# Layer 1's values directly behind its scores, inside the second unit of layer 2's values

## The chip, the core and the metric

The kernel runs on one core of a Trainium2 chip. Its time is the device time in microseconds (us) of one execution, and the numbers compared are medians of several executions. Engines are named as in the profile: PE is TensorE's matmul, PEld its weight load, DVE is VectorE, ACT is ScalarE, POOL is GpSimd and SP is SyncE. L1234 is line 1234 of the kernel.

## What is computed

The input x has four images of 64x64 positions with 64 channels. Four attention layers follow each other, each over the 4096 positions of an image. Layer 1, which the change touches, has few channels in its scores (8) and its values (32), and its keys and values are pooled to 1024 positions:

```python
# layer 0: attention over 4096 keys, 64 channels
x = gamma * softmax(q @ k) ... + x
# layer 1
theta = x @ sn(w_theta)                     # 4096 x 8
phi   = maxpool2(x @ sn(w_phi))             # 1024 x 8
attn  = softmax(theta @ phi.T)              # 4096 x 1024
g     = maxpool2(x @ sn(w_g))               # 1024 x 32
x     = x + sigma * ((attn @ g) @ sn(w_o) + b_o)
# layer 2: group norm, attention over 4096 keys, projection, + x
# layer 3: group norm, attention over 4096 keys, projection, + normed x
```

sn divides a weight matrix by an estimate of its largest singular value. All is float32. The softmax is computed as exponentials of the scores, values times exponentials, and a division by the sum of the exponentials.

## The kernel before

Of each image, the core holds arrays of 128 partitions: two halves of the positions by 64 channels. Layers 0, 2 and 3 are written as a sequence of *steps*. The big attention of the foreground gives each step two *units*. A unit is 128x1024 scores, built by four matmuls in 64x64 corners of TensorE (`first`, L1199 for layers 2 and 3, L971 for layer 0), their exponentials on ScalarE (L1204), their sums into `zacc` on VectorE (L1210), and two or more steps later the values times exponentials (`then`, L1234 for layers 2 and 3), again four matmuls, into two PSUM accumulators. A chunk of 512 queries has 32 units j = 0..31; there are four chunks, so 64 steps.

Everything else is background work in small pieces. It is a Python generator that yields the *place* it wants for its next piece, and `step` lets it go on at that place. A step issues its instructions in this order:

- the two score units of the foreground;
- the first unit of values;
- place MID: one piece of background work, or a piece of urgent work of the foreground itself;
- the second unit of values; if the background waits for place LATE, this unit is split into query columns 0 to 255 and 256 to 511, and the background's piece goes between them. For j = 0 and j = 31 `parts` doesn't split: the piece goes behind the whole unit;
- the functions in the list `later` (VectorE work put off to here);
- place END.

A place ALONE takes the MID slot and keeps LATE empty for that step. [...]

Layer 1 is such background work. `layer1(on, st, bank)` runs for image 0 beside layer 0 with `bank` False, and for images 1, 2 and 3 beside layer 2 of the image before with `bank` True. In both cases it goes through 16 units (j, k): two halves j of the queries, eight blocks k of 128 keys. For unit n:

- `scores(j, k)` takes two score tiles, fills them with eight matmuls of 8 rows by 64 columns of the array (L1079), and issues two exponentials on ScalarE (L1085). It returns a function `accumulate` that adds both to the sums on VectorE (L1094).
- `add(j, k)` multiplies the pooled values with the exponentials of that unit: four matmuls of 128 rows by 32 columns (L1105), into one PSUM accumulator over the eight k where `bank` is True. At k = 7 ScalarE copies the accumulator out (L1116).
- behind `add` of the last k of the first half, `finish(0)` starts with `normalise`: four matmuls sum the exponentials over partitions (L1121), ScalarE copies that out (L1127), and reciprocals (L1130) and a product follow in pieces at MID.

A unit's scores go at LATE, and the values of the unit before it at END of the same step. Score tiles come from a pool of two [...], shared by foreground and background; the PSUM accumulators from a pool of four; the exponentials from a pool of 14.

Of the kernel before, what the change touches and what calls it, by code (L numbers as in the profile page):

```python
# [597 lines left out]
def fast_path(tc: tile.TileContext, a: dict, out: bass.AP, bad):  # L598
# [21 lines left out]
    MID, ALONE, LATE, END = range(4)  # L620
# [153 lines left out]
    later = []  # L774
# [256 lines left out]
    def layer1(on, st, bank):  # L1031
# [39 lines left out]
        def scores(j, k):  # L1071

            ss = [s_tile() for e in range(2)]
            n, d = divmod(k, 2)
            for m in range(2):
                for e in range(2):
                    for i in range(2):
                        r = slice((2 * e + i) * 32, (2 * e + i) * 32 + D8)
                        nc.tensor.matmul(  # L1079
                            ss[e][half(m), chunk(i)], pgs[0 if e == d else 1][r, ds(n * P + m * C, C)],  # L1080
                            th[r, chunk(2 * j + i)], start=True, stop=True,
                        )
            ps[j, k] = pk = [p_tile() for e in range(2)]
            for e in range(2):
                nc.scalar.activation(pk[e], ss[e], AF.Exp)  # L1085
            if k == 0:
                return lambda: None
            if k == 1:
                zaccs[j] = x_tile("zacc1").rearrange("p (e f) -> p e f", e=2)
            zs = [ps[j, 0][e] if k == 1 else zaccs[j][:, e, :] for e in range(2)]  # L1090

            def accumulate():
                for e in range(2):
                    nc.vector.tensor_tensor(zaccs[j][:, e, :], zs[e], pk[e], ALU.add)  # L1094

            return accumulate

        def add(j, k):
            if k == (NK - 1 if bank else 0):
                os[j] = o_tile("o1")  # L1100
            if k == 0 and bank:
                accs[j] = acc_tile()
            acc = accs[j] if bank else s_tile()[:, 0:512]
            for q in range(4):
                nc.tensor.matmul(  # L1105
                    acc[quarter(q), :], g[:, k, :], ps[j, k][q // 2][:, chunk(q % 2)],
                    start=(k == 0 or not bank), stop=(k == NK - 1 or not bank),
                )
            if k > 0:
                del ps[j, k]  # L1110
            if k == 1:
                del ps[j, 0]
            if not bank and k > 0:
                nc.vector.tensor_tensor(os[j], os[j], acc, ALU.add)
            elif not bank or k == NK - 1:
                nc.scalar.copy(os[j], acc)  # L1116
# [27 lines left out]
        def finish(j):  # L1144

            if not bank:
                yield ALONE
            yield from normalise(j)
            yield MID
            yield ALONE  # L1150
            last(j)

        end = None
        todo = [(j, k) for j in range(2) for k in range(NK)]
        for n in range(len(todo) + 1):
            accumulate = None
            if n < len(todo):
                yield LATE
                accumulate = scores(*todo[n])
            if n:  # L1160
                yield END
                add(*todo[n - 1])
            if accumulate:
                accumulate()
            if n == NK:
                end = finish(0)
                at = next(end)
            elif end is not None:
                yield at
                at = next(end, None)  # L1170
                end = end if at is not None else None
# [535 lines left out]
    layer0(s0)  # L1707
    drain()
    background(3.0, layer1("DVE", s0, False), before2("DVE", s0))
    free = layer0(s1)  # L1710
    drain()
    background(3.0, layer1("ACT", s1, True), before0("ACT", s2))
    free = layer2(s0, free)
    drain()
    background(1.0, before2("DVE", s1), loads(s3))
    free = layer0(s2)
    drain()
    background(3.0, layer1("ACT", s2, True), before0("ACT", s3))
    free = layer2(s1, free)
    drain()  # L1720
# [97 lines left out]
```

## Time and profile before

| what | value |
|---|---|
| median of 3 runs | 3004.53 us (3003.02 to 3005.59) |
| the profiled execution | 3005.78 us |
| its span, first to last instruction | 3003.7 us |
| TensorE clock granted, mean | 0.999 |
| layer 1 scores L1079 beside layer 2 start at | 586.64, 1096.44, 1606.23 us |
| VectorE busy from 584 to 700 us | 92.84 of 116 us |
| ScalarE busy from 584 to 700 us | 75.40 of 116 us |

The span is cut by the foreground: layer 0 of image 0 first, then a turn of layer 2 or 3 of one image and layer 0 of another. The part with layer 1 beside layer 2 is about 105 us long and comes three times. Within it TensorE's records follow each other almost without idle time (115.29 us of 116 between 584 and 700).

How to read the timeline of TensorE: one line is a run of equal instructions, with the start, the length, the line of the kernel, what is written and read, the shape and the number of records. Every matmul of this kernel leaves two records of its shape. The length of a line [...] overlaps the next line; differences between starts are the times that blocks take.

### The profile page before, as it was taken

How to read it: one execution, taken by the hardware profiler on the slowest of the kernel's cores; microseconds unless marked ns; L12 is line 12 of the kernel's file. 1: busy time of each engine (PE TensorE's matmuls, PEld its weight loads, DVE VectorE, ACT ScalarE, POOL GpSimd, SP SyncE). 2: the span in 40 equal slices, each digit the busy share in tenths (PEclk: the TensorE clock that was granted, in tenths of full speed). 3: DMA queues.
4: the chain of work that ended last, by engine and by line, in shares of the span. 5: the costliest groups of instructions: out<-in, count | busy, mean ns of one | idle time of the engine just before them, and what ended most of it. 6: DMA issues, size and time to landing. Idle time of an engine off the chain costs nothing.

```text
span 3003.7 us, 64700 instructions
## 1 busy us (share of the span) xinstructions
PE 2979.2 (99%) x28509; PEld 1133.0 (38%) x28509; DVE 1760.1 (59%) x2003; ACT 1943.8 (65%) x2816; POOL 34.1 (1%) x32
## 2 busy tenths in 40 slices
PE   9999999999999999999999999999999999999998
PEld 4333233433444433344443333333343334333333
DVE  1211332587731068772017887777887777877777
ACT  6877778666588866557886655655555655555554
POOL 0000000000000000000000000000000000000000
PEclk9999999999999999999999999999999999999999
DMA  2010000000001000000000000000000000000000
GB/s 37 2 29 5 1 1 2 19 2 1 15 1 29 1 5 1 15 2 10 7 2 5 2 8 9 19 5 8 5 19 6 17 1 1 12 12 5 9 5 9
DMA packets 42081, 25.79 MB, mean 9 GB/s; under 512 B 39872, under 2 KB 39872, under 8 KB 40384
## 3 DMA queue, kind: packets, MB, share of 16 engines
q1 hardware_dynamic: 40080, 21.17, 3.7%
q8 instruction: 225, 3.69, 0.5%
q10 hardware_dynamic: 1712, 0.41, 0.1%
q14 instruction: 64, 0.52, 0.1%
HBM read 4.79 MB, written 4.19 MB: 3 GB/s over the span
## 4 chain that ended last, share of the span: by engine, by line
PE 98%; ACT 1%; SPq 0%; DVE 0%; issue 0%; DMA 0%; ACTq 0%; DVEq 0%
PE acc L1234 30%; PE s L1199 30%; PE acc L996 15%; PE s L971 14%; PE s L1079 2%; PE acc L1105 1%; ACT p L1085 1%; PE s L883 1%; PE s L1105 1%; PE s L1262 1%; PE s L1346 0%; PE s L902 0%; PE s L1260 0%; PE s L1443 0%; PE s L1366 0%; PE s L1051 0%
## 5 line engine op out<-in xcount | busy, mean ns | idle before, releaser
L1204 ACT ACTIVATE p<-s 128x1024 f32<-128x1024 f32 x1024 | 994.8, 1022 | 705.6 <-PE s L1199 694.0
L1210 DVE TENSOR_TENSOR zacc<-zacc,p 128x1024 f32<-128x1024 f32 x960 | 1174.1, 1223 | 372.2 <-ACT p L1204 334.4
L975 ACT ACTIVATE p<-s 128x1024 f32<-128x1024 f32 x512 | 519.9, 1016 | 42.7 <-PE s L971 24.3
L1234 PE MATMUL acc<-p,v 64*64 64x512 f32 (+1 forms) x4456 | 525.2, 558 | 0.0
L996 PE MATMUL acc<-p,vs 64*64 64x512 f32 (+1 forms) x4224 | 512.2, 578 | 0.5 <-ACT vs L985 0.5
L1199 PE MATMUL s<-q,k 64*64 64x512 f32 x2048 | 495.5, 593 | 2.1 <-ACT p L1085 2.1
L1234 PE MATMUL acc<-p,hT 64*64 64x512 f32 x4096 | 494.1, 590 | 0.0
L971 PE MATMUL s<-xT,q 64*64 64x512 f32 x2048 | 487.4, 591 | 2.5 <-DVE v L903 0.6
L971 PE MATMUL s<-xT,q_swapped 64*64 64x512 f32 x2048 | 488.4, 591 | 0.0
L1199 PE MATMUL s<-q,xT 64*64 64x512 f32 x2048 | 486.9, 589 | 0.0
L1199 PE MATMUL s<-q,h_swapped 64*64 64x512 f32 x2048 | 479.4, 589 | 0.0
L1199 PE MATMUL s<-q,k_swapped 64*64 64x512 f32 x2048 | 477.6, 593 | 0.0
L977 DVE TENSOR_REDUCE all_z<-z 128x1 f32<-128x4 f32 x128 | 20.1, 157 | 643.2 <-ACT p L975 643.2
L1234 PEld LDWEIGHTS acc<-p,v 64*64 64x64 f32 x4456 | 179.9, 133 | 285.0 <-issue 280.0
L996 PEld LDWEIGHTS acc<-p,vs 64*64 64x64 f32 x4224 | 176.3, 133 | 270.3 <-issue 206.5
L985 ACT ACTIVATE vs<-v,all_r 64x64 f32<-64x64 f32 x512 | 177.2, 346 | 145.2 <-PE acc L996 72.4
L1234 PEld LDWEIGHTS acc<-p,hT 64*64 64x64 f32 x4096 | 156.7, 133 | 263.8 <-issue 263.1
L971 PEld LDWEIGHTS s<-xT,q_swapped 64*64 64x64 f32 x2048 | 145.8, 133 | 146.3 <-issue 114.2
L1199 PEld LDWEIGHTS s<-q,h_swapped 64*64 64x64 f32 x2048 | 143.9, 133 | 141.2 <-issue 135.5
L971 PEld LDWEIGHTS s<-xT,q 64*64 64x64 f32 x2048 | 145.8, 133 | 134.1 <-issue 106.0
L1199 PEld LDWEIGHTS s<-q,xT 64*64 64x64 f32 x2048 | 143.4, 133 | 140.1 <-issue 137.7
L1199 PEld LDWEIGHTS s<-q,k 64*64 64x64 f32 x2048 | 140.1, 132 | 148.3 <-issue 100.2
(233 smaller groups left out, 1560.2 us busy)
## 6 DMA issues: line engine op xcount, KB each, us to landing
k_swapped<-k SPq DMA_DIRECT2D x8, 512.0 KB, 6.0
h_swapped<-xT SPq DMA_DIRECT2D x8, 512.0 KB, 5.3
out_dram<-turned SPq DMA_DIRECT2D x62, 64.0 KB, 1.9
xin<-in_x_dram SPq DMA_DIRECT2D x24, 128.0 KB, 5.0
q_swapped<-q SPq DMA_DIRECT2D x6, 512.0 KB, 5.4
pg<-pg SPq DMA_DIRECT2D x8, 128.0 KB, 2.3
xin<-in_x_dram SPq DMA_DIRECT2D x12, 64.0 KB, 2.3
xin<-in_x_dram ACTq DMA_DIRECT2D x4, 64.0 KB, 2.6
```

Of the source, the lines that this page charges most:

```text
L883: nc.tensor.matmul(bank[i][half(e), :], w[half(i), half(e)], rhs[half(i), chunk(2 * j + (1 - e if exchanged else e))], start=True, stop=True,)
L971: nc.tensor.matmul(s[half(e), chunk(i)], queries(m, i, e), k[half(i), chunk(c)], start=True, stop=True)
L975: nc.scalar.activation(p, s, AF.Exp, accum_out=zs[m][:, c : c + 1])
L985: nc.scalar.activation(vs[half(e), :], v[half(e), m, :], AF.Copy, scale=rz[half(e), m : m + 1])
L996: nc.tensor.matmul(acc[c][half(i), cols], vs[half(e), :], ps[2 * t + n][half(e), chunk(i)][:, cols], start=(m == 0 and e == 0), stop=(m == ...
L1079: nc.tensor.matmul(ss[e][half(m), chunk(i)], pgs[0 if e == d else 1][r, ds(n * P + m * C, C)], th[r, chunk(2 * j + i)], start=True, stop=True,
L1085: nc.scalar.activation(pk[e], ss[e], AF.Exp)
L1105: nc.tensor.matmul(acc[quarter(q), :], g[:, k, :], ps[j, k][q // 2][:, chunk(q % 2)], start=(k == 0 or not bank), stop=(k == NK - 1 or not ...
L1199: nc.tensor.matmul(s[half(e), chunk(i)], k[(j + i) % 2][half(i), ds(j // 2 * P + e * C, C)], q[half(i), chunk(c)], start=True, stop=True,)
L1204: nc.scalar.activation(p, s, AF.Exp)
L1210: add = lambda: nc.vector.tensor_tensor(zaccs[c], p0, p, ALU.add)
L1234: nc.tensor.matmul(accs[c][e][half(i), cols], v[half(e), j, :], p[half(e), chunk(i)][:, cols], start=(j == 0), stop=(j == NB - 1),)
```

## The change

```diff
@@ layer1
         for n in range(len(todo) + 1):
             accumulate = None
             if n < len(todo):
                 yield LATE
                 accumulate = scores(*todo[n])
             if n:
-                yield END
+                if not bank:
+                    yield END
+                elif n == len(todo):
+                    yield LATE
                 add(*todo[n - 1])
-            if accumulate:
+            if accumulate and bank:
+                later.append(accumulate)
+            elif accumulate:
                 accumulate()
             if n == NK:
                 end = finish(0)
                 at = next(end)
```

Where `bank` is True, the values of unit n - 1 (`add`) are issued right behind the scores of unit n, at the same LATE, so between the two parts of the second unit's values, and no longer at END. The last unit's values, which have no scores ahead of them, ask for a LATE of their own. The accumulation of the exponentials goes into `later`, which the same step works off behind the second unit's values. With `add` of unit 7, the start of `finish(0)` moves from END to LATE as well. Where `bank` is False, nothing changes.

## The prediction

> **What bounds the kernel now.** I read the page first, its busy table and the chain that ended last.
>
> ```profile
> PE 2979.2 (99%) x28509; PEld 1133.0 (38%) x28509; DVE 1760.1 (59%) x2003; ACT 1943.8 (65%) x2816; POOL 34.1 (1%) x32
> ...
> PE 98%; ACT 1%; SPq 0%; DVE 0%; issue 0%; DMA 0%; ACTq 0%; DVEq 0%
> ```
>
> TensorE is busy 99% of the span and is 98% of the chain. So a rearrangement elsewhere is worth nothing, and even on TensorE nothing is won by filling idle time. What can change is the time that TensorE loses while it counts as busy. To see that, I read the timeline of TensorE over one step that carries a piece of layer 1 beside layer 2. Columns: start, length, instructions. The lengths overlap, so I take differences of starts.
>
> ```profile
> 659.41 1.11 PE L1079 MATMUL s<-th,pg 8*64 8x512 f32 x16
> 660.46 0.66 PE L1234 MATMUL acc<-p,v 64*64 64x256 f32 x8
> 661.05 1.06 PE L1105 MATMUL acc<-p,pg 128*32 128x512 f32 x8
> 662.05 0.65 PE L1199 MATMUL s<-q,k 64*64 64x512 f32 x2
> ...
> 663.81 1.47 PE L1234 MATMUL acc<-p,v 64*64 64x512 f32 x16
> 665.21 1.15 PE L1079 MATMUL s<-th,pg 8*64 8x512 f32 x16
> ```
>
> From one layer 1 score block to the next: 1.05 (scores) + 0.59 (rest of the second unit's values) + 1.00 (layer 1's values) + 1.76 (two score units of layer 2) + 1.40 (the first unit's values and half of the second's) = 5.80 us. The lines give each matmul as two records. Eight such 64x64 records of 512 columns with nothing of another shape around them take 0.86 us (649.56 to 650.42), and the sixteen of two units 1.72 us (697.08 to 698.80). By that measure the five blocks would take 0.86 + 0.43 + 0.86 + 1.72 + 1.29 = 5.16. The missing 0.64 us sits at the borders between tile shapes: 8*64, 64*64, 128*32 and 64*64 again, with four borders a step.
>
> Then two other places of the same timeline. In the first, 128*32 is followed by 64*64 values; in the second the layer 1 scores are followed directly by layer 1's values, because there the second unit is the last of its chunk and isn't split.
>
> ```profile
> 693.46 1.07 PE L1121 MATMUL acc<-zacc,ones 128*32 128x512 f32 x8
> 694.46 1.09 PE L1234 MATMUL acc<-p,v 64*64 64x512 f32 x8
> 695.37 0.60 PE L1199 MATMUL s<-q,k 64*64 64x512 f32 x2
> ...
> 627.36 1.11 PE L1079 MATMUL s<-th,pg 8*64 8x512 f32 x16
> 628.40 1.07 PE L1105 MATMUL acc<-p,pg 128*32 128x512 f32 x8
> 629.62 0.65 PE L1199 MATMUL s<-q,k 64*64 64x512 f32 x2 [0.15 <-ACT p L1085]
> ```
>
> Last, what releases TensorE after a layer 1 score block: the timelines of weight loads and of ScalarE in the next step, and the weight loads and VectorE where layer 1 sums its first half's denominators.
>
> ```profile
> 668.46 0.14 PEld L1199 LDWEIGHTS s<-q,k_swapped 64*64 64x64 f32 x2 [0.38 <-ACT p L1085]
> ...
> 666.47 1.94 ACT L1085 ACTIVATE p<-s 128x1024 f32<-128x1024 f32 x2 [1.27 <-PE s L1079]
> ```
>
> ```profile
> 634.94 0.12 PEld L1121 LDWEIGHTS acc<-zacc,ones 128*32 128x32 f32 x2 [0.30 <-issue]
> ...
> 635.14 0.11 PEld L1121 LDWEIGHTS acc<-zacc,ones 128*32 128x32 f32 x2
> ...
> 633.87 1.22 DVE L1094 TENSOR_TENSOR zacc<-zacc,p 128x1024 f32<-128x1024 f32 x1
> ```
>
> The second score unit's weights (668.46) go out just as the second layer 1 exponential ends (666.47 + 1.94 = 668.41). And the last two of the denominators' weight loads (635.14) go out just after the last layer 1 accumulation ends (633.87 + 1.22 = 635.09): that wait is already near its point.
>
> [...] a border costs 0.10 to 0.19 us, no border nothing. [...] within one shape (the weight loads for the layer 2 values run 0.43 us ahead of their matmuls, 663.39 against 663.81), and shows none of it over a border: the load for L1105 starts at 661.05 with its matmul. [...]
>
> **The change part by part.**
>
> 1. *Layer 1's values move from the step's end to directly behind the scores.* What moves is four matmuls (eight records); in one step an image ScalarE's copy L1116 goes with them, behind the same two exponentials as before; nothing of it is on SP's or POOL's queue, and no DMA. No instruction is added or removed in a normal step. TensorE's order was values-half, scores, values-half, layer 1 values, next scores of layer 2; it becomes values-half, scores, layer 1 values, values-half, next scores. The borders go from four to three, since the last two blocks now have one shape. With rows from above: scores before 128*32, 1.04 (627.36 to 628.40); 128*32 before 64*64 values, 1.00 (693.46 to 694.46); the half behind it, 0.43 plus the 0.05 to 0.06 by which the block at 694.46 exceeds 0.86, so 0.49; two score units without a border ahead, 1.71 (695.37 to 697.08); and 1.40. Sum 5.64 to 5.65: 0.15 us less a step.
>
> 2. *How many steps.* Each image has 16 layer 1 units of scores, so 15 steps with both scores and values. One of them (627.36) has the unsplit second unit, and its order on TensorE stays as it is. One (632.85) also starts the denominators and goes by itself below. That leaves 13. Images 1, 2 and 3 run layer 1 beside layer 2 (first score blocks at 586.64, 1096.44, 1606.23, with the same steps): 39 steps x 0.15 = 5.85 us less. Layer 1 of image 0, beside layer 0, keeps its order.
>
> 3. *The last values wait for LATE, not END.* That step (687.05: 1.82, 1.00, 1.77) now splits the second unit: 1.40 + 1.00 + 0.49 + 1.71 = 4.60 against 4.59. Four matmuls more, nothing in time.
>
> 4. *The denominators' matmuls of the first half (L1121) move forward with the values.* They were issued at 635.37 (632.85 + 1.04 + 0.60 + 0.88). Without the 0.60 they would start at 634.77, but the accumulation they read ends at 635.09, and their last two weight loads can't go before 635.14. VectorE can't be earlier: it waits at 631.00 for ScalarE's copy of layer 2's accumulator, and then works without a gap to 635.09. So TensorE stands some 0.36 us. From 635.14: 1.00 to the half, 0.49, 1.71 gives 638.34 to 638.35 against 638.11 in the trace: 0.24 us later, three times, 0.72 us more. Behind the waiting instruction TensorE's queue holds the half of layer 2's values and the next scores; those feed ScalarE, which has its copies L1116 and L1127 to do in that time and slack behind them.
>
> 5. *Accumulations go through the list of later work instead of directly.* They come behind that list's other entries as before, in the same step: VectorE's order doesn't change. Cost nothing. Its cover: steps with a reciprocal hold about 5.55 us of VectorE work in 5.80 (idle 0.20 to 0.24), and would still fit in 5.65. If they didn't, only the accumulators would lag, which TensorE reads much later.
>
> 6. *ScalarE's releases.* The next score pair's first unit needs the first exponential, out at 2.26 us after the layer 1 scores begin (627.36 to 629.62, where it did bind). In the new order it is wanted at 1.04 + 1.00 + 0.49 = 2.53. The second unit's weights are released at 3.25 at the latest (665.21 to 668.46) and its matmuls are wanted at 2.53 + 0.86 = 3.39; a load takes 0.14. So the cover is just enough. If it isn't, the cost is the 0.06 us of the step at 629.62 (1.83 instead of 1.77): 39 x 0.06 = 2.3 us at most. Below nothing isn't possible for this term. I take nothing.
>
> Sum: -5.85 + 0.72 = -5.1 us. The profiled execution took 3005.78 (span 3003.7 and 2.1 around it) and would take 3000.6; its time is 1.25 over the median of 3004.53, so as a median I forecast 2999.4. That is 0.17% less, and what a measurement of this kernel can tell from no change is about 0.2%, or 6.0 us.
>
> **The rivals.**
>
> *A larger gain.* If the accumulation is ready for the denominators after all (a wait of nothing makes that step gain 0.14) and a border is worth 0.165, as the shortest readings of each block give: 42 x 0.165 = 6.9, so 2997.6. For it: the borders read from 0.10 to 0.19. Against it: the load at 635.14.
>
> [...] The half unit behind layer 1's values is only 0.43 us long, and may not hide the weights of the scores behind it, or the exponentials' release takes 0.06 back and more. Then the gain is 0 to 2 us, less the 0.72: about 3004. For it: the cover in part 6 is thin. Against it: the half is as long as the 0.43 by which loads run ahead.
>
> *Slower: ScalarE's second exponential becomes the gate of every step.* Place: the weights of the second score unit of layer 2, released by L1085. It decides once that release comes later than 3.39 + 0.15 = 3.54 us after the layer 1 scores begin; up to there it eats the gain, beyond it adds. At 3.75 each of the 39 steps would lose 0.21: 8.2 + 0.7 = 9 us, so 3013. For it: PEld's longest waits at L1199 name just this release. Against it: ScalarE's pair starts 1.2 to 1.26 after the scores' begin and takes 1.94, and neither changes.
>
> That the edit leaves the order as it is can be left out: where the unit is split, the place of the values differs.
>
> **How the numbers follow.** Forecast (3.5 to 6 us less): 0.62. Larger gain: 0.20. [...] Slower: 0.07. The forecast's own width reaches over the 6.0 us bound with some 0.05 of its chance: faster 0.25, within 0.2% 0.68 (the rest of the forecast [...]), slower 0.07. The range runs from the larger gain with 0.3 us of scatter, 2997.3, [...], 3003.9, and leaves the slower case and little else out.
>
> **What would show it.** In the trace after: L1105 directly behind L1079 at 1.04; a 256-column L1234 block behind it of 0.49, then L1199 at 1.71 to 1.72; 5.65 from score block to score block in 13 steps an image; a wait of L1121 for VectorE of about 0.36 in each image; and no TensorE wait for L1085 in the 13 steps. Wrong would be: steps of 5.80 or more, or idle time of TensorE before L1199.

## The result, and the profile after

| | median, us | lowest to highest | runs |
|---|---|---|---|
| before | 3005.10 | 3002.75 to 3005.88 | 22 |
| changed | 2999.90 | 2997.99 to 3000.39 | 22 |

The ratio of changed to before is 0.9983, with a 95% interval of 0.9977 to 0.9990. The change takes 5.2 us off; by the interval it is between 3.0 and 6.9. The slowest run of the changed kernel (3000.39) lies below the fastest of the kernel before (3002.75). The profiled execution took 2999.91 us, with a span of 2997.8.

The page of the changed kernel, its busy table and the chain that ended last, gives nearly the same shares as before. The 24 records more on TensorE are the four matmuls more in the last step of each of three images, two records each. Lines behind L1165 have moved by five: L1234 is now L1239, L1199 is L1204.

```profile
PE 2973.8 (99%) x28533; PEld 1138.8 (38%) x28533; DVE 1759.9 (59%) x2003; ACT 1942.9 (65%) x2816; POOL 34.1 (1%) x32
...
PE 98%; ACT 1%; DVE 0%; issue 0%; DMA 0%; ACTq 0%; DVEq 0%
```

TensorE's timeline over the step that answers to the one shown of before (start, length, engine, line, operation):

```profile
658.62 1.11 PE L1079 MATMUL s<-th,pg 8*64 8x512 f32 x16
659.67 1.06 PE L1105 MATMUL acc<-p,pg 128*32 128x512 f32 x8
660.66 0.66 PE L1239 MATMUL acc<-p,v 64*64 64x256 f32 x8
661.15 0.60 PE L1204 MATMUL s<-q,k 64*64 64x512 f32 x2
...
662.87 1.47 PE L1239 MATMUL acc<-p,v 64*64 64x512 f32 x16
664.26 1.15 PE L1079 MATMUL s<-th,pg 8*64 8x512 f32 x16
```

By differences of starts: 1.05 + 0.99 + 0.49 + 1.72 + 1.39 = 5.64 us, where it was 5.80. Layer 1's values (L1105) take what they took. The half of layer 2's values behind them fell from 0.59 to 0.49 and the score pair from 1.76 to 1.72: these two blocks have one shape and nothing between them any more. The step as a whole is 0.16 us shorter; the rest is in the last digits of the other blocks.

The step with the denominators of the first half, on TensorE: first L1121 and what follows it in the kernel before, then the changed kernel, then weight loads of the changed kernel.

```profile
635.37 1.04 PE L1121 MATMUL acc<-zacc,ones 128*32 128x512 f32 x8
636.34 0.65 PE L1199 MATMUL s<-q,k 64*64 64x512 f32 x2
```

```profile
632.11 1.12 PE L1079 MATMUL s<-th,pg 8*64 8x512 f32 x16
633.15 1.07 PE L1105 MATMUL acc<-p,pg 128*32 128x512 f32 x8
634.04 1.42 PE L1121 MATMUL acc<-zacc,ones 128*32 128x512 f32 x8
635.38 0.66 PE L1239 MATMUL acc<-p,v 64*64 64x256 f32 x8
635.87 0.60 PE L1204 MATMUL s<-q,k 64*64 64x512 f32 x2
```

```profile
634.40 0.14 PEld L1121 LDWEIGHTS acc<-zacc,ones 128*32 128x32 f32 x4 [0.24 <-DVE zacc L1094]
635.38 0.21 PEld L1239 LDWEIGHTS acc<-p,v 64*64 64x64 f32 x8 [0.84 <-issue]
635.65 0.14 PEld L1204 LDWEIGHTS s<-q,k 64*64 64x64 f32 x2
```

L1121 takes 1.34 us (634.04 to 635.38) instead of 0.97 (635.37 to 636.34), and the bracket names VectorE's accumulation L1094 as what its weights waited for. This step costs more than before.

From the first layer 1 scores to the end of the second half's denominators each image took 107.82, 107.82 and 107.80 us before, and takes 106.00, 105.96 and 105.96 now: 1.84 us less on the mean, three times, 5.5 us. The two profiled executions are 5.87 apart and the medians 5.2. What differs from the 5.5 lies outside these stretches, where both kernels issue the same, and is taken as scatter: the first of these layer 1 scores start at 586.64 us before, at 586.87 in the changed kernel and at 587.28 in e5, which issues the same up to there.

### The profile page after: what moved, and what is told of

Same layout as the page of the kernel before. It is cut to its first block, busy times and chain, and to the rows that moved or that the text cites. A ratio compares the mean times of both kernels' runs of the same rounds, so it can differ in the third digit from the quotient of the medians.

```text
span 2997.8 us, 64742 instructions
## 1 busy us (share of the span) xinstructions
PE 2973.8 (99%) x28533; PEld 1138.8 (38%) x28533; DVE 1759.9 (59%) x2003; ACT 1942.9 (65%) x2816; POOL 34.1 (1%) x32
## 4 chain that ended last, share of the span: by engine, by line
PE 98%; ACT 1%; DVE 0%; issue 0%; DMA 0%; ACTq 0%; DVEq 0%
PE acc L1239 30%; PE s L1204 29%; PE s L971 15%; PE acc L996 15%; PE s L1079 2%; PE acc L1105 1%; ACT p L1085 1%; PE s L883 1%; PE s L1105 1%; PE s L1267 1%; PE s L902 1%; PE s L1351 0%; PE s L1265 0%; PE s L1448 0%; PE s L1140 0%; PE s L1371 0%
## 5 line engine op out<-in xcount | busy, mean ns | idle before, releaser
L1239 PE MATMUL acc<-p,v 64*64 64x512 f32 (+1 forms) x4480 | 526.0, 556 | 0.0
L1204 PE MATMUL s<-q,k 64*64 64x512 f32 x2048 | 493.2, 591 | 2.1 <-ACT p L1085 2.1
L1239 PE MATMUL acc<-p,hT 64*64 64x512 f32 x4096 | 494.2, 590 | 0.0
L1204 PE MATMUL s<-q,xT 64*64 64x512 f32 x2048 | 486.9, 589 | 0.0
L1204 PE MATMUL s<-q,h_swapped 64*64 64x512 f32 x2048 | 479.4, 589 | 0.0
L1204 PE MATMUL s<-q,k_swapped 64*64 64x512 f32 x2048 | 475.2, 590 | 0.0
L1239 PEld LDWEIGHTS acc<-p,v 64*64 64x64 f32 x4480 | 180.6, 133 | 288.6 <-issue 283.7
L1239 PEld LDWEIGHTS acc<-p,hT 64*64 64x64 f32 x4096 | 156.7, 133 | 263.8 <-issue 263.1
L1204 PEld LDWEIGHTS s<-q,h_swapped 64*64 64x64 f32 x2048 | 144.0, 133 | 141.2 <-issue 135.5
L1204 PEld LDWEIGHTS s<-q,k_swapped 64*64 64x64 f32 x2048 | 143.1, 133 | 142.7 <-issue 100.1
L1204 PEld LDWEIGHTS s<-q,xT 64*64 64x64 f32 x2048 | 143.4, 133 | 140.1 <-issue 137.7
```

What stands on the lines that cost most here:

```text
L1204: nc.tensor.matmul(s[half(e), chunk(i)], k[(j + i) % 2][half(i), ds(j // 2 * P + e * C, C)], q[half(i), chunk(c)], start=True, stop=True,)
L1239: nc.tensor.matmul(accs[c][e][half(i), cols], v[half(e), j, :], p[half(e), chunk(i)][:, cols], start=(j == 0), stop=(j == NB - 1),)
```

## The experiments

Each was measured beside runs of the kernel before on the same chip (3005.4 to 3005.6 us); ratios are to those. The changed kernel was not run beside them. Where they are compared with its 2999.90, keep in mind that the kernel before was 0.3 to 0.5 us slower beside them than beside it (3005.10); the comparisons of blocks within the traces don't depend on that.

**e1: the accumulation at once, in every step.**

```diff
-            if accumulate and bank:
-                later.append(accumulate)
-            elif accumulate:
+            if accumulate:
                 accumulate()
```

> The changed kernel, but the accumulation of the layer 1 exponentials (L1094) is issued at once behind layer 1's values, inside LATE, and not through the list of later work. It then stands on VectorE ahead of layer 2's odd sum and, in the step with the unsplit unit, ahead of the sum that waits for ScalarE's copy of layer 2's accumulator. Theory (the denominators' matmuls wait for VectorE, which has the accumulation last in line): the wait of L1121 goes, the step with the denominators falls from 5.47 to about 5.12 us, 3 x 0.35 = 1.05 us less than the changed kernel, so about 2998.9. The other steps stay at 5.64. Rival (the route through the later list is needed to keep VectorE out of TensorE's way): VectorE stands idle for the exponentials in every step and falls behind, steps grow over 5.64, the time rises.

Measured: 3001.70 us, ratio 0.9987 (0.9981 to 0.9994). The denominators' step came out as the theory has it: L1121 takes 0.97 (634.21 to 635.18), the step 5.10. The ordinary steps stay at 5.64, so the order on TensorE alone gives their gain. Yet the whole is some 2 us slower than the changed kernel, not 1 us faster: the forecast of 2998.9 missed. TensorE's timeline has the loss in another place, some 17 us later:

```profile
649.99 0.60 PE L1202 MATMUL s<-q,k 64*64 64x512 f32 x2
...
651.51 0.65 PE L1202 MATMUL s<-q,k_swapped 64*64 64x512 f32 x2 [0.91 <-DVE xT L1392]
```

The second score unit stands 0.91 us for L1392, layer 2's update on VectorE, which holds the score tile that the unit needs. VectorE's own timeline says why it is late; first e1, then the changed kernel:

```profile
645.39 2.36 DVE L1094 TENSOR_TENSOR zacc<-p 128x1024 f32<-128x1024 f32 x2 [1.92 <-ACT p L1085]
647.67 2.55 DVE L1213 TENSOR_TENSOR zacc<-zacc,p 128x1024 f32<-128x1024 f32 x2
650.14 1.23 DVE L1392 SCALAR_TENSOR_TENSOR xT<-s,bp,xT 128x256 f32<-128x256 f32 x2
```

```profile
642.39 2.56 DVE L1215 TENSOR_TENSOR zacc<-zacc,p 128x1024 f32<-128x1024 f32 x2 [0.67 <-ACT p L1209]
649.22 1.31 DVE L1394 SCALAR_TENSOR_TENSOR xT<-s,bp,xT 128x256 f32<-128x256 f32 x2
```

VectorE stood 1.92 us for the layer 1 exponentials. Queued behind them was layer 2's odd sum (L1213): the sum for the second, odd unit of a step, which the kernel puts into the list of later work. In the changed kernel that sum is done in this time (by 644.95), and the update starts 5.87 us after the step's layer 1 scores (643.35 to 649.22); in e1 it is 7.00 (643.14 to 650.14). The score pair behind the update takes 2.83, 2.89 and 2.92 us in the three images of e1, against 1.82, 1.78 and 1.78 in the changed kernel. So the theory was right for its step, 0.37 us less, but it had left out this place, 1.0 to 1.1 us more. The rival had the cause right, VectorE idle for the exponentials, and not the extent: it expected longer steps everywhere, and the loss sits in one place of each image. The list of later work isn't just tidiness.

**e2, e3: layer 1's values a piece away from its scores.** The second unit's values were cut into columns 0 to 255, 256 to 383 and 384 to 511, and the background was called at both cuts. In e3, layer 1 also asks for LATE a second time ahead of its values. Excerpt:

```diff
+        elif thrice:
+            yield slice(0, 256)
+            within()
+            yield slice(256, 384)
+            within()
+            yield slice(384, 512)
...
             if n:                     # e3 alone
-                yield END
+                if not bank:
+                    yield END
+                else:
+                    yield LATE
                 add(*todo[n - 1])
```

> The changed kernel with the second unit's values in three pieces where they are split: columns 0 to 255, then layer 1's scores and values, then 256 to 383, then 384 to 511. It is the control for e3: no border between tile shapes more than in the changed kernel. Theory (only borders between shapes cost): 5.64 us a step and 2999.9 as the changed kernel. Rival (pieces of 128 columns are too short for their weight loads of 0.14 us): 0.1 us a step more, 4 us.

> As e2, but layer 1's values go between the pieces 256 to 383 and 384 to 511 of the second unit's values. Layer 2's next scores still follow layer 2's values, so nothing but the count of borders differs from e2: four instead of three. Theory (a border between tile shapes costs 0.15 us wherever it is): 5.80 us a step, 39 x 0.155 = 6.0 over e2, less 3 x 0.2 for the denominators, which come 0.37 later and wait no more: about 3005.3, and the gain of the change is gone. Rival (the gain comes from taking layer 1's values away from the place right ahead of layer 2's scores): as e2, 2999.9 or less.

Measured: e2 3026.88 (ratio 1.0068, 1.0054 to 1.0081), e3 3046.82 (1.0136, 1.0120 to 1.0151). Both missed, since in most of its steps neither is the kernel that was meant. In e2 the second call took the next unit's scores into the same step, and these took 1.79 us (599.70 to 601.49) instead of 1.04: they waited for their score tiles. Over the whole run the weight loads of layer 1's scores stood 14.7 us, in 30 waits, for layer 1's exponentials (L1091 there), which read these tiles; in the kernel before they stood for none of them. In e3 the pieces came in the other order, values ahead of scores, as its timeline shows:

```profile
605.39 1.06 PE L1113 MATMUL acc<-p,pg 128*32 128x512 f32 x8
606.39 0.45 PE L1247 MATMUL acc<-p,v 64*64 64x128 f32 x8
606.77 1.11 PE L1087 MATMUL s<-th,pg 8*64 8x512 f32 x16
607.81 0.45 PE L1247 MATMUL acc<-p,v 64*64 64x128 f32 x8
609.03 0.65 PE L1212 MATMUL s<-q,k 64*64 64x512 f32 x2 [0.77 <-ACT p L1093]
```

That makes e3 a test of something else: with only 128 columns of values between layer 1's scores and layer 2's, layer 2's scores start 2.26 us after layer 1's (606.77 to 609.03) and TensorE stands 0.77 of it for the exponentials. In this step, what follows layer 1's scores must fill these 2.26 us. Later in the image both kernels do have the order that was meant, and there the theory holds: a step of e2 takes 5.65 us (632.01 to 637.66), a step of e3 5.80 (667.36 to 673.16).

**e4: no split.**

```diff
-                yield LATE
+                yield END if bank else LATE
                 accumulate = scores(*todo[n])
             if n:
                 if not bank:
                     yield END
                 elif n == len(todo):
-                    yield LATE
+                    yield END
                 add(*todo[n - 1])
```

The accumulation follows directly, at END.

> The changed kernel with layer 1's scores and values both at END, behind the whole second unit of layer 2's values: again three borders between shapes, but nothing between layer 1's values and layer 2's next scores. Theory (the half unit behind layer 1's values is what covers the exponentials, as the step with the unsplit unit shows: 2.26 us from the layer 1 scores to layer 2's, against 2.53): each of 39 steps becomes 5.92 instead of 5.64, with a TensorE wait for L1085 of 0.15: 39 x 0.28 + 0.2 = 11 us over the changed kernel, about 3011. Rival (the count of borders alone decides): 2999.9.

Measured: 3012.43 us, ratio 1.0023 (1.0014 to 1.0033); 7 us over before and 12.5 over the changed kernel. The ordinary steps have what the theory took from the one unsplit step, 5.91 to 5.92 us:

```profile
599.30 1.11 PE L1079 MATMUL s<-th,pg 8*64 8x512 f32 x16
600.34 1.06 PE L1105 MATMUL acc<-p,pg 128*32 128x512 f32 x8
601.56 0.65 PE L1202 MATMUL s<-q,k 64*64 64x512 f32 x2 [0.16 <-ACT p L1085]
```

Again 2.26 us from scores to scores, of which TensorE stands 0.16 for the exponentials. So the count of borders decides only as long as the half unit is there to cover the exponentials.

**e5: the accumulation at once in one step only.**

```diff
-            if accumulate and bank:
+            if accumulate and bank and n != NK - 1:
                 later.append(accumulate)
```

> The changed kernel, but only the accumulation of the last key block of the first half (unit n = 7) is issued at once, behind layer 1's values inside LATE; all others go through the list of later work. Theory (e1 won 0.37 us in the step with the denominators and lost 1.0 us in the step with layer 2's update, where VectorE was late with L1392 because the accumulation stood ahead of it): the denominators' step is 5.10 us, the step after layer 2's update stays at 1.82 us for its score pair, and the whole is 3 x 0.37 = 1.1 us less than the changed kernel: 2998.8, some 2.5 us less than e1. Rival (e1's loss comes from the direct accumulation in every step): at or over the changed kernel's 2999.9.

Measured: 2998.92 us, ratio 0.9978 (0.9969 to 0.9986). TensorE in the denominators' step:

```profile
633.57 1.07 PE L1105 MATMUL acc<-p,pg 128*32 128x512 f32 x8
634.45 1.04 PE L1121 MATMUL acc<-zacc,ones 128*32 128x512 f32 x8
635.42 0.66 PE L1239 MATMUL acc<-p,v 64*64 64x256 f32 x8
```

L1121 is back at 0.97, and the score pair behind layer 2's update takes 1.75. The stretches of the three images are 105.56, 105.71 and 105.55 us, 0.44, 0.25 and 0.41 less than in the changed kernel, 1.1 in all. The medians differ by 1.0 as well, but the intervals of the two ratios overlap; the verdict rests on the stretches of one traced execution each. This version has the lowest median of the study, 6.7 us below the kernel before beside it.

**e6: only the list of later work, in the kernel before.** The accumulation is appended to `later` right behind the scores, and `add` stays at END.

```diff
+            if accumulate and bank:
+                later.append(accumulate)
             if n:
                 yield END
                 add(*todo[n - 1])
-            if accumulate:
+            if accumulate and not bank:
                 accumulate()
```

> The kernel before, with one part of the change: the accumulation of the layer 1 exponentials goes into the list of later work; layer 1's values stay at END, and so do the denominators. Theory (only the order on TensorE matters): steps of 5.80 us, no wait of L1121, the time of the kernel before, 3005.1 to 3005.4. Rival (part of the gain comes from VectorE's order): 1 us or more less than the kernel before.

Measured: 3005.70 us, ratio 1.0001 (0.9993 to 1.0009). TensorE's step is that of before, 1.04 + 0.59 + 1.00 + 1.77 + 1.40 = 5.80:

```profile
604.13 1.11 PE L1079 MATMUL s<-th,pg 8*64 8x512 f32 x16
605.17 0.66 PE L1236 MATMUL acc<-p,v 64*64 64x256 f32 x8
605.76 1.06 PE L1105 MATMUL acc<-p,pg 128*32 128x512 f32 x8
606.76 0.65 PE L1201 MATMUL s<-q,k 64*64 64x512 f32 x2
```

This part of the change alone brings nothing that could be measured.

**e7, e8: the same number of pieces, with and without one border more.** In both the unit's values are cut three ways. In e7 the second cut calls nothing; in e8 it calls a place of its own, AGAIN, at which only layer 1's values wait. Excerpt:

```diff
+        elif thrice:
+            yield slice(0, 256)
+            within()
+            yield slice(256, 384)
+            within(AGAIN)          # e8 alone
+            yield slice(384, 512)
...
+                else:
+                    later.append(accumulate)
+                    yield AGAIN    # e8 alone
                 add(*todo[n - 1])
```

> The control for e8, in place of e2, whose second call inside the unit took a second layer 1 unit into the same step. The changed kernel with the second unit's values in columns 0 to 255, then layer 1's scores and values, then 256 to 383, then 384 to 511. Theory (only borders between tile shapes cost): 5.64 us a step, 2999.9 as the changed kernel. Rival (pieces of 128 columns are too short for their weight loads of 0.14 us): 0.1 us a step more, so 3004.

> As e7, but layer 1's values stand between the pieces 256 to 383 and 384 to 511: one border more than e7 in each of 39 steps, while layer 2's next scores follow layer 2's values as in e7. Theory (a border costs about 0.15 us wherever it is): 5.80 us a step, of it 0.38 for the piece between scores and values and 0.27 for the last; 39 x 0.155 = 6.0 over e7, less 3 x 0.37 because the denominators come 0.38 later and wait no more: e7 plus 5, about 3005. Rival (the gain of the change comes from what follows layer 1's values, not from the count of borders): as e7.

Measured: e7 3000.32 us, ratio 0.9982 (0.9974 to 0.9990); e8 3005.96 us, ratio 1.0001 (0.9993 to 1.0010). First e7, then e8:

```profile
603.88 1.11 PE L1084 MATMUL s<-th,pg 8*64 8x512 f32 x16
604.92 1.06 PE L1110 MATMUL acc<-p,pg 128*32 128x512 f32 x8
605.92 0.67 PE L1244 MATMUL acc<-p,v 64*64 64x128 f32 x16
606.40 0.60 PE L1209 MATMUL s<-q,k 64*64 64x512 f32 x2
```

```profile
604.15 1.11 PE L1087 MATMUL s<-th,pg 8*64 8x512 f32 x16
605.19 0.45 PE L1248 MATMUL acc<-p,v 64*64 64x128 f32 x8
605.57 1.07 PE L1113 MATMUL acc<-p,pg 128*32 128x512 f32 x8
606.57 0.45 PE L1248 MATMUL acc<-p,v 64*64 64x128 f32 x8
606.84 0.60 PE L1213 MATMUL s<-q,k 64*64 64x512 f32 x2
```

From layer 1's scores to layer 2's it is 2.52 in e7 and 2.69 in e8, and the rest of the step is alike. One border more a step puts the time back at that of before, even with the denominators' wait gone (0.97 for L1129 in e8). In e8 layer 2's scores still follow layer 2's values, and still the gain is lost: it comes from the number of borders, not from who stands ahead of the scores. What TensorE does in the time that a border costs, e7 and e8 don't show.

## Why the prediction was right

The forecast was 5.1 us less than before, and 5.2 were measured. The mechanism came as forecast; that the two agree to 0.1 us is in part luck, since the interval is 3.9 us wide and the three stretches alone give 5.5. Of the forecast's terms, the steps gave 0.16 us each where 0.15 was taken, and the denominators took back 0.21 an image where 0.24 was taken. The forecast held 6.0 us for the least that a measurement can tell from no change; with 22 runs of each kernel, 5.2 us can be told. Point by point:

1. *Three borders instead of four.* Right. The step was put together from blocks measured at other places of the trace of before and came to 5.64 to 5.65; it is 5.64. e8 takes the gain away by adding a border alone. The runs show that a change of tile shape costs TensorE time here, and give its price, 0.16 to 0.17 us (5.80 less 5.64; 2.69 less 2.52). What TensorE does in that time was not shown: the first weight load behind a border starts with its matmul (L1239, both at 635.38), and no run tells how much of the price that is. The forecast read its borders as 0.10 to 0.19 us; by its own blocks the time over the undisturbed one is 0.19, 0.16, 0.14, 0.04 and 0.11, so only the mean of 0.16 a border stands. The undisturbed time of the layer 1 scores among them, 0.86, is assumed, as nothing shows that block without borders.
2. *Thirteen steps an image.* Right. The step with the unsplit unit is as before (1.04 and 1.22 for L1079 and L1105).
3. *The last values' own LATE.* Right: 1.40 + 1.00 + 0.48 + 1.72 = 4.60 from 685.45.
4. *The wait of the denominators.* Right in kind and close in size: the step went from 5.26 to 5.47, 0.21 more, where 0.24 was forecast. That VectorE can't be earlier holds only for its order there: e1 and e5 issue the accumulation sooner, the wait goes, and the step falls to 5.10.
5. *The list of later work costs nothing.* Right: e6 shows no cost that could be measured. The score pair behind layer 2's update took 1.76 to 1.77 us before, 1.78 to 1.82 in the changed kernel and 1.82 to 1.83 in e6, but 1.75 to 1.77 in e7, which uses the list too. So some 0.05 us an image comes and goes there, and the runs don't show that the list is its cause. What the forecast didn't say is how much hangs on this place: e1 shows 1 us an image when the accumulation stands ahead of the odd sum.
6. *ScalarE's releases.* Right: layer 2's second score unit isn't held. In the changed kernel its weights and the exponentials are

```profile
667.51 0.14 PEld L1204 LDWEIGHTS s<-q,k_swapped 64*64 64x64 f32 x2 [0.54 <-ACT p L1085]
...
665.52 1.94 ACT L1085 ACTIVATE p<-s 128x1024 f32<-128x1024 f32 x2 [1.27 <-PE s L1079]
```

The weights go out 3.25 us after the scores (664.26), as before, and the first of their matmuls starts at 667.68, 0.17 us later. Over the 39 steps this distance is 0.14 to 0.20 us, and the load takes up to 0.14: the cover is just enough, as forecast, and the score pair takes 1.71 to 1.72 us in all of them. The bracket names L1085 for idle time of the weight load alone, which cost nothing.

Of the rivals, the larger gain needed the denominators to be free of the wait; e5 made them so. Its gain is 6.7 us against the kernel before beside it (3005.62) and 6.6 by the stretches, close to the 6.9 of that case; its 2998.9 looks short of the 2997.6 only because that was counted from a lower base, 3004.53. The case of about 3004 (given 0.11), with the half unit behind layer 1's values too short for what follows it, did not come: that half takes 0.48 to 0.49 us and the score pair behind it 1.71 to 1.72. Nor did the gate at the second exponential. e3 and e4 show a gate at ScalarE (TensorE stood 0.77 and 0.16 us for it in the steps shown), though at the first exponential, 2.26 us behind the scores; the changed order stays about 0.27 clear of it (658.62 to 661.15 is 2.53).

The median of before turned out 0.6 us higher in 22 runs than in the three shown, and that of the changed kernel 0.5 over the 2999.4 forecast; that is the base, not the change.

## What to carry to other kernels

- Where TensorE is busy all the time, read the differences between the starts of its blocks, and compare a block's time with that of the same block amid others of its shape. Here, what was left over sat at the borders between tile shapes, and each border saved was worth about 0.16 us, as long as the new order still covered what TensorE waits for (e4 doesn't).
- A new order can be priced before it is built by taking each block, with its neighbours' shapes, from another place of the same trace. Then look for what moves earlier along with it: here the denominators' matmuls, which read a sum before it was ready, cost 0.37 us an image, a sixth of the 2.2 us that an image gains without that wait (e5).
- VectorE took its instructions in the order of issue here: in e1 the accumulation stood 1.92 us for ScalarE and started at 645.39, and the odd sum issued behind it only at 647.67. So putting a waiting instruction a little earlier moved the wait to what was issued behind it. Advance the one instruction whose reader waits (e5), not all of its kind.

## What the runs showed of the hardware

- A border's price was nearly the same for pieces of 128 and of 256 columns, 0.17 and 0.16 us. With a border on both sides, the 256 columns took 0.59 us in the kernel before, 0.16 over an undisturbed 0.43, and the 128 columns 0.38 in e8, 0.17 over 0.21. (The 0.43 and 0.21 are estimates: a half and a quarter of the 0.86 us of an undisturbed unit.) Cutting alone cost nothing here: two pieces of 128 took 0.48 us in e7 (605.92 to 606.40), and one of 256 took 0.48 in the changed kernel (666.34 to 666.82).
- In e8 most of the price fell behind a block, by an estimate. There the last piece, with a border only ahead of it, takes 0.27 us, 0.06 over its estimated 0.21. That leaves about 0.11 of the 0.17 for the border behind. It agrees with the block ahead of the second half's denominators in the kernel before, with a border only behind it: 0.97 us (692.49 to 693.46), 0.11 over 0.86.
- No weight load ran ahead over a border. In the changed kernel from 580 to 700 us, the first load of a block behind a border starts within 0.01 us of the block's first matmul, at all 56 borders (L1239 at 635.38, for one). Within one shape the loads did run ahead (L1204 at 635.65 for the matmul at 635.87, 0.22 us). How much of a border's price this is stays open.
